# Placing a set's slots one turn later in a graph-layer kernel on one Trainium2 core

## The chip, the cores and the metric

The kernel runs on one core of one Trainium2 chip. The metric is the time of one execution on the device in microseconds (us), the median of several runs. Beside those runs one execution was taken with the hardware profiler; its rows are what the working uses.

## The reference

A graph layer of 12,500 nodes with 128 features and 400,000 edges, sorted by the node that they end in, followed by a residual sum and a normalisation:

```
Xs = X[src]
m_data = Xs @ W_data.T + b_data
m_ctrl = Xs @ W_control.T + b_control
msg = jnp.where((edge_types == 0)[:, None], m_data, m_ctrl)
agg = jax.ops.segment_sum(msg, dst, num_segments=X.shape[0])
out = relu(agg + (X @ W_self.T + b_self))
x = layernorm(x + out)
```

The kernel adds the rows of x per node and edge type first, and multiplies by the weights afterwards.

## The kernel before

The 3,125 columns of 128 edges are cut into 25 groups (g) of 125 columns, and each group into five pairs of windows. The short window of a pair ("p", 5 columns, once 25) fetches its source rows from DRAM by GpSimd's indirect DMAs (L725). The long one ("e", 20 columns, 2,560 edges) fetches nothing: x lies in SBUF as three bf16 parts (x3), and TensorE picks the rows with one-hot matrices. The loop at L1010 makes one step for each of the 113 e-windows ("sets", w).

Picking needs a table of slots: for each of 100 cells (blocks of 128 nodes) up to 32 edges. `give_slots` (L523) makes it for one set:

- VectorE (DVE) builds the one-hot block matrix O (L531) and sums of it (`fours`, L547, L548); TensorE adds them along the lanes into the PSUM tile rk (`before`, L555); VectorE makes the rank of each edge within its cell (`ranks`, L565 to L580), and from it a one-hot rank matrix times node and code, rv (`rank_matrix`, L603 to L607).
- `put` (L614) places the slots: 20 matmuls of O and rv into rk (L619).
- `spread` (L624) casts rk to bf16 on ScalarE (ACT; tile cell, L627), writes its 100 x 32 node part to DRAM (tile there, L629) and reads it back into all 128 partitions (tile pick, 800 KB, L631). Both transfers go through SyncE's queue (SP).
- `turn_codes` and `keep_codes` (L636 to L650) move the code part into the tile code, by small matmuls from cell (L639) and one ScalarE cast (L649). With them goes the third and fourth part of `spare_slots`, for the few edges that found no slot (L507, L514 to L518).

rk has one buffer, so the next set's `before` can begin when `keep_codes` has read it. pick has two, one in use and one being filled. VectorE then turns pick into the one-hot matrix in place, in two halves (`pick_matrix`, L661).

A step of the loop holds six turns (`unit(t)`, t = 0 to 5, in `picked`, L823) for its own set w. Turn t picks 4 x 128 rows in 16 matmuls each for two PSUM tiles (got, L790), which ScalarE casts to emsg (L802); VectorE makes the one-hot matrix of codes (esel, L784); TensorE counts (L814) and adds the rows of the turn before into the window's sums (L821, shown as L676). The last turn, t = 5, also picks the last rows (L808, into the tile fin or got) and counts the last five. At the end of a turn it runs `tiled.get(t)`, which are parts of the set w + 2; those under 6 run in `end`, which is called in turn 0 of the next step. Other work is merged into the step by due times: `before` in turn 1, `ranks` at 0.26, `rank_matrix` at 0.3, the block matrix of set w + 3 at 0.55, `pick_matrix` of set w + 1 at 0.6 and 0.65, p-windows, loads, and about once in four to five steps the `finish` of an earlier group (fp32 products L918, normalisation on VectorE, L947 on ScalarE, output L950, and reads of x rows, L890).

The framework's scheduler takes the instructions in that order as priorities and fixes at build time in which order each engine gets them; an engine works in its own order and waits by semaphore. The order in the trace differs from the listed one where the scheduler saw a gap: the first half of pick_matrix (L661) usually stands between L569 and L574 of `ranks`, though it is listed after both.

Of the kernel before, what the change touches and what calls it, by code (L numbers as in the profile page):

```python
# [150 lines left out]
def short_path(ctx, tc, const, ident, eps, wT, brow, bad, x, src, dst, etype, ws, bs, out):  # L151
# [371 lines left out]
    def give_slots(w):  # L523
        g, i = each_e[w]
        blk, blk2, node2, code2, pk = (t[:, i * EC:(i + 1) * EC] for t in codes["e", g])
        s = {}
# [122 lines left out]
            nc.scalar.copy(code, at.to_broadcast(list(code.shape)))  # L649
            s["spares"][3]()  # L650

        s["tiled"] = {4: [put, spread], 6: [turn_codes, keep_codes]}
        return s, [(0.58, block_matrix), (0.6, fours), (0.66, same_lane)], [
            (0.1, before), (0.26, ranks), (0.28, lambda: s["spares"][1]()), (0.3, rank_matrix), (0.75, over),
        ]
# [302 lines left out]
    def last_spares():  # L958
        s = spare_slots(pairs - 1, ps1.tile([P, 512], FP, name="rk"))
        return {6: s[2:]}, [(0.1, s[0]), (0.28, s[1])]  # L960

    def begin_slots(w):
        slots[w], a, b = give_slots(w)
        begun[w] = b
        return [u for _, u in a]
# [44 lines left out]
    for w in range(pairs):  # L1010
# [9 lines left out]
        tiled, begin = {}, []  # L1020
        if w + 2 < pairs:
            tiled, begin = slots[w + 2]["tiled"], begun.pop(w + 2)
        elif w + 2 == pairs:
            tiled, begin = last_spares()
# [184 lines left out]
```

## Time and profile before

| | before |
|---|---|
| median of 3 runs | 1956.54 us (1954.3 to 1966.5) |
| profiled execution, own time | 1946.23 us |
| its span, first to last instruction | 1944.4 us |
| mean granted TensorE clock | 0.986 |
| TensorE matmul (PE) busy | 1753.1 us, 90% |
| TensorE weight load (PEld) busy | 1354.9 us, 70% |
| VectorE (DVE) busy | 1717.1 us, 88% |
| GpSimd (POOL) busy | 1362.6 us, 70% |
| ScalarE (ACT) busy | 1303.0 us, 67% |
| DMA, mean | 131 GB/s |

The busy shares in 40 slices are even from the third slice to the last but one: the main loop fills the span. A row of the groups or of the timeline gives line, engine, operation, tiles written and read, and shape; "idle" or the bracket at the end of a row is how long the engine stood before it, and what released it. SPq is SyncE's queue, on which DMAs are issued.

### The profile page before, as it was taken

What the parts mean: (1) busy time and instruction counts of PE and PEld (TensorE: products, weight loads), DVE (VectorE), ACT (ScalarE), POOL (GpSimd) and SP (SyncE); (2) the same over time, 40 slices, a digit from 0 to 9 for tenths busy, and PEclk for the clock granted to TensorE, in tenths of its full rate; (3) what the DMA queues carried; (4) which work ended last, traced back from release to release, by engine and by line L of the source; (5) the groups of instructions that cost most, each with busy time, mean ns of one, the idle gap of its engine ahead of it and who ended that gap; (6) DMA issues with size and microseconds to landing.
All of it is one profiled execution on the core that took longest, in us unless ns stands there. A gap on an engine that the chain in (4) does not pass through costs nothing.

```text
span 1944.4 us, 75191 instructions
## 1 busy us (share of the span) xinstructions
PE 1753.1 (90%) x30869; PEld 1354.9 (70%) x30869; DVE 1717.1 (88%) x4707; ACT 1303.0 (67%) x2464; POOL 1362.6 (70%) x996
## 2 busy tenths in 40 slices
PE   0669999999999999999999999999999999999996
PEld 0457777677777776777777777777777777777775
DVE  7969999999899888999999889989989889888883
ACT  4646776676676676676676667667676666766765
POOL 0378768777788777667777667787787667777760
PEclk9989999999999999999999999999999999999998
DMA  7734443443543443443444434444434344444331
GB/s 210 227 94 129 134 148 108 144 147 101 149 141 107 145 136 110 145 136 115 140 136 119 123 129 119 143 127 126 144 129 146 114 128 144 117 136 135 115 111 35
DMA packets 186533, 254.91 MB, mean 131 GB/s; under 512 B 85369, under 2 KB 152995, under 8 KB 183108
## 3 DMA queue, kind: packets, MB, share of 16 engines
q1 hardware_dynamic: 128418, 152.97, 24.6%
q0 software_dynamic: 45136, 90.65, 16.5%
q10 hardware_dynamic: 12626, 6.40, 1.2%
q8 instruction: 243, 3.98, 0.8%
q14 instruction: 110, 0.90, 0.1%
HBM read 231.89 MB, written 18.04 MB: 129 GB/s over the span
## 4 chain that ended last, share of the span: by engine, by line
DVE 53%; PE 30%; DMA 10%; issue 3%; ACT 2%; DVEq 1%; SPq 1%; POOL 0%; ACTq 0%
PE sums L676 13%; PE got L790 8%; DMA pick<-there 7%; DVE esel L481 6%; DVE pick L661 6%; DVE prod L569 5%; DVE rv L607 4%; DVE found L578 3%; DVE prod L547 3%; PE rk L619 3%; DVE half L574 3%; DVE ahead L565 3%; DVE rm L481 2%; DVE half L575 2%; DVE prod L548 2%
## 5 line engine op out<-in xcount | busy, mean ns | idle before, releaser
L725 POOL DMA_INDIRECT msg<-rows,pidx x865 | 1212.8, 1402 | 376.8 <-PE got L790 163.0
L802 ACT CAST emsg<-got 128x768 bf16<-128x768 f32 x1356 | 1026.9, 803 | 356.5 <-PE got L790 337.0
L676 PE MATMUL sums<-esel,emsg 128*128 128x176 bf16 x8136 | 748.2, 241 | 0.0
L676 PEld LDWEIGHTS <-emsg 128*128 128x128 bf16 x8136 | 596.2, 98 | 156.0 <-issue 143.2
L790 PE MATMUL got<-x,pick 128*32 128x384 bf16 x10896 | 611.6, 331 | 12.6 <-ACT emsg L802 10.1
L790 PEld LDWEIGHTS <-pick 128*32 128x32 bf16 x11074 | 250.0, 96 | 125.3 <-issue 20.3
L481 DVE TENSOR_TENSOR esel<-code_col,code 128x1408 bf16<-128x1408 bf16 x339 | 309.0, 912 | 8.8 <-PE sums L676 3.2
L769 POOL DMA_INDIRECT last<-rows,idx x113 | 145.7, 1289 | 171.7 <-DMA bias<-b_parts 70.9
L676 PE MATMUL sums<-psel,msg 128*128 128x48 bf16 x2595 | 184.9, 185 | 7.3 <-DVE acc L714 5.1
L714 DVE TENSOR_TENSOR acc<-acc,sums 128x352 f32 (+2 forms) x238 | 101.4, 426 | 96.9 <-PE sums L676 81.6
L619 PE MATMUL rk<-rv,O 128*128 128x64 bf16 x2260 | 89.6, 195 | 103.3 <-DVE rv L607 103.0
L619 PEld LDWEIGHTS <-O 128*128 128x128 bf16 x2260 | 86.1, 100 | 127.8 <-issue 126.6
L814 PE MATMUL sums<-esel,one_col 128*32 128x176 bf16 x2825 | 169.5, 242 | 2.1 <-DVE esel L481 1.2
L676 PEld LDWEIGHTS <-msg 128*128 128x128 bf16 x2595 | 149.2, 97 | 15.9 <-issue 13.3
L661 DVE TENSOR_SCALAR pick<-pick,lane_f 128x1600 bf16<-128x1600 bf16 x226 | 144.1, 643 | 17.0 <-DMA pick<-there 16.5
L761 PE MATMUL sums<-psel,one_col 128*128 128x48 bf16 x865 | 145.3, 183 | 0.0
L481 DVE TENSOR_TENSOR O<-cell_col,blk 128x2000 bf16<-128x2000 bf16 x113 | 134.2, 1188 | 4.9 <-issue 2.5
L569 DVE TENSOR_TENSOR prod<-O,ahead 128x2000 bf16<-128x2000 bf16 x113 | 134.1, 1187 | 0.0
L814 PEld LDWEIGHTS <-one_col 128*32 128x32 bf16 x2825 | 80.9, 96 | 34.0 <-issue 2.2
L565 DVE TENSOR_REDUCE ahead<-rk 128x100 bf16<-128x500 f32 x113 | 76.0, 673 | 12.0 <-PE rk L497 9.0
L627 ACT CAST cell<-rk 128x64 bf16<-128x64 f32 x113 | 23.9, 212 | 87.9 <-PE rk L619 79.1
L761 PEld LDWEIGHTS <-one_col 128*128 128x128 bf16 x865 | 82.8, 96 | 0.0
(173 smaller groups left out, 2077.0 us busy)
## 6 DMA issues: line engine op xcount, KB each, us to landing
pick<-there SPq DMA_DIRECT2D x113, 800.0 KB
acc<-acc_start SPq DMA_DIRECT2D x23, 1280.0 KB
msg<-rows,pidx POOLq DMA_INDIRECT x865
rows<-x SPq DMA_DIRECT2D x6, 1344.0 KB
xs<-in_x_dram SPq DMA_DIRECT2D x99, 62.5 KB
out_dram<-h SPq DMA_DIRECT2D x99, 62.5 KB
xt<-in_x_dram ACTq DMA_DIRECT2D x6, 896.0 KB
there<-cell SPq DMA_DIRECT2D x113, 6.2 KB
```

Source lines behind the costliest of these rows:

```text
L481: nc.vector.tensor_tensor(sel.rearrange("p n (w t) -> p n w t", t=2), col[:rows].rearrange("p (o w t) -> p o w t", o=1, t=2).to_broadcast( ...
L565: nc.vector.tensor_reduce(ahead, s["rk"][:, :CQ * NCELL].rearrange("p (c j) -> p j c", j=NCELL), AX.X, OP.add)
L569: nc.vector.tensor_tensor(prod, s["O"], ahead.rearrange("p (o j) -> p o j", o=1).to_broadcast([P, EC, NCELL]), op=OP.mult)
L619: nc.tensor.matmul(s["rk"][:m, :2 * CAP], s["held"][:, c * NCELL:c * NCELL + m], s["rv"][:, c].rearrange("p v r -> p (v r)"), start=(c == ...
L661: nc.vector.tensor_scalar(t, t, lane_f, None, op0=OP.is_equal)
L676: nc.tensor.matmul(out, msg[:, j * D:(j + 1) * D], sel, start=(start and j == 0), stop=stop, skip_group_check=True)
L725: return nc.gpsimd.indirect_dma_start(out=msg, out_offset=None, in_=rows3[:, :], in_offset=bass.IndirectOffsetOnAxis(ap=codes["p", g][0][: ...
L761: nc.tensor.matmul(cnt, one_col, sel, start=False, stop=(c == n - 1), skip_group_check=True)
L769: return nc.gpsimd.indirect_dma_start(out=msg[:OVF, :], out_offset=None, in_=rows3[:, :], in_offset=bass.IndirectOffsetOnAxis(ap=slots[w][ ...
L790: last = nc.tensor.matmul(ps[CAP * a:CAP * (a + 1), :], slots[w]["pick"][:, a * NQ + q, :], x3[:, 4 * q + a - a0].rearrange("p j d -> p (j ...
L802: nc.scalar.copy(msg, ps[:, :, :3 * D])
L814: nc.tensor.matmul(cells_of(s["ps"], EW, 1)[CAP * (q % 4):CAP * (q % 4 + 1), :], one_col[:, :CAP], s["sel"][q], start=(q < 4), stop=(q + 4 ...
```

## The change

`put` and `spread` of set w + 2 are run at the end of turn 5 of step w instead of turn 4. In the listed order they come after the picking, counting, last rows and adding of turn 5 and no longer before them. Nothing else is changed, and no instruction is added or dropped.

```diff
-        s["tiled"] = {4: [put, spread], 6: [turn_codes, keep_codes]}
+        s["tiled"] = {5: [put, spread], 6: [turn_codes, keep_codes]}
```

The parts that it moves, as they stand:

```python
        def put():
            for c in range(EC):
                m = P if c < EC - 1 else NCELL
                nc.tensor.matmul(
                    s["rk"][:m, :2 * CAP], s["held"][:, c * NCELL:c * NCELL + m], s["rv"][:, c].rearrange("p v r -> p (v r)"),
                    start=(c == 0), stop=(c == EC - 1), skip_group_check=True,
                )

        def spread():
            cell = s["cell"] = two.tile([P, 2 * CAP], BF, name="cell")
            nc.scalar.copy(cell, s["rk"][:, :2 * CAP])
            there = scr.tile([NCELL, CAP], BF, name="there")
            nc.sync.dma_start(out=there[:, :], in_=cell[:NCELL, :CAP])
            pick = s["pick"] = two.tile([P, NCELL, CAP], BF, name="pick")
            nc.sync.dma_start(
                out=pick.rearrange("p j r -> p (j r)"),
                in_=there.rearrange("(o j) r -> o (j r)", o=1).to_broadcast([P, NCELL * CAP]),
            )
```

## The prediction, made before the result was known

> **What bounds the kernel now.** I read the page first. Its engine rows and the chain that ended last say that neither TensorE nor VectorE rules alone:
>
> ```profile
> PE 1753.1 (90%) x30869; PEld 1354.9 (70%) x30869; DVE 1717.1 (88%) x4707; ACT 1303.0 (67%) x2464; POOL 1362.6 (70%) x996
> DVE 53%; PE 30%; DMA 10%; issue 3%; ACT 2%; DVEq 1%; SPq 1%; POOL 0%; ACTq 0%
> ```
>
> Two engines at about 90% that hold the chain in turn are two that wait for each other. The list of waits (who waited for whom: total us, times, longest) names the places:
>
> ```profile
> PE rk L619 <- DVE rv L607: 103.0, 83, 19.0
> DVE acc L714 <- PE sums L676: 81.6, 62, 13.5
> DVE pick L661 <- DMA pick<-there: 16.5, 22, 2.2
> ```
>
> TensorE stands before `put` until VectorE has made rv; VectorE stands before `accumulate` until TensorE has closed the sums; and VectorE stands a little for the transferred pick. The first and the third row are the two ends of the moved step. The chain of waits in order of time shows how they lie in one ordinary step (start, us, what):
>
> ```profile
> 1842.15 0.81 DVE rv L607 x2
> 1842.97 0.04 issue
> 1843.01 0.76 PE rk L619 x20
> 1843.77 0.19 PE got L790
> 1843.96 0.23 PE sums L814 x8
> 1844.20 0.16 PE fin L790 x2
> 1844.36 1.09 PE sums L676 x15
> ...
> 1848.99 0.34 PE rk L555 x4
> 1849.33 0.05 PE rk L497
> 1849.38 0.02 issue
> 1849.40 0.68 DVE ahead L565
> ```
>
> So a step is two phases: VectorE from `ahead` to rv, then TensorE from rv to the next `ahead`. In the second one `put` stands first, and behind it in TensorE's queue comes the rest of turn 5: three got, eight counts, the two last rows, twelve sums. That is 0.19 + 0.23 + 0.16 + 1.09 = 1.67 us of work which needs neither rv nor `put`, behind an instruction that waits for rv (0.80 us in this step).
>
> Last I lined up all 113 sets from the timeline: end of rv, start of put, issue of pick, the last of pick's 128 packets of 6,400 bytes, first half of pick_matrix. Leaving out the first four sets, where the start lies, and the last, there are two kinds. In 84 ordinary sets put stands in TensorE's queue in the middle or at the end of turn 5's got matmuls and TensorE waits there, 72.2 us in all, 0.86 a set; the step takes 15.1 us (median). In 24 sets the fp32 products of `finish` hold TensorE up, put comes 2.3 us after rv with no wait, and the step takes 20.1 us. One of those:
>
> ```profile
> 1012.66 0.76 PE L619 MATMUL rk<-rv,O 128*128 128x64 bf16 x20
> 1013.46 0.21 ACT L627 CAST cell<-rk 128x64 bf16<-128x64 f32 x1 [0.21 <-PE rk L619]
> 1017.15 0.35 SPq L631 DMA_DIRECT2D pick<-there  x1
> 1019.30 2.62 SPq L192 DMA_DIRECT2D esrc<-in_src_dram  x1
> 1024.00 0.64 DVE L661 TENSOR_SCALAR pick<-pick,lane_f 128x1600 bf16<-128x1600 bf16 x1 [0.66 <-DMA pick<-there]
> ```
>
> Here VectorE does stand for pick (last row, 0.66 us), though it was issued before the loads of the next group (L192).
>
> **The change, part by part.** *Put on TensorE.* Nothing is added. The 20 matmuls (0.76 us) go behind 1.67 us of turn 5. Per set TensorE saves the wait, as far as it is under 1.67 us, and VectorE gains only if it then really stood for TensorE in that phase. The smaller of the two, taken set by set (wait before put; VectorE's idle time before L714, L518 and L565), sums to 45 us over the 84 sets, 0.53 each. Its ends: 0, if the scheduler keeps put where it is, and 68 us, if every wait under 1.67 us turns into time. In the other 24 sets there is no wait to save: 0.
>
> *Spread on ScalarE.* One cast of 0.21 us goes behind the cast of the last rows (0.47 us) and perhaps one of emsg (0.80 us). In a few sets it already starts 0.8 us late. On `turn_codes` it has no effect: after put come turn 0's 16 got (0.76 us) and 15 sums (1.24 us) before L639 wants cell, which is 2.0 us of cover against 0.3 for the cast. For pick it costs 0 to 0.8 us.
>
> *Spread's transfers on SP.* From the start of put to pick's last packet it takes 7.2 us (median of the ordinary sets; 1.6 of it from there to pick's issue, 4.2 from that issue to the last packet); the first halving starts 8.9 us after put. Less 0.35 us, the smallest time seen between last packet and halving, 1.3 us are free (median; under that in 42 of the 84). The change eats them from both sides: put starts later by 1.6 less the wait, 0.79 us on average, and the halving wants to start 0.53 us sooner. If VectorE's order stays as it is, it stands 30 us over the 84 sets, leaving 15 of the 45.
>
> In the 24 finish sets put falls behind all of turn 5, since it stood ahead of turn 5's got: from its end to the end of those twelve sums are 2.7 us (median). Pick has next to nothing free there, so with VectorE's order unchanged it stands 57 us more. A bound below is 0, if the halving is seated later. A bound above is 103 us, if pick falls behind the loads on SP too (4.6 us a set, from two issues of esrc of 2.62 and 1.95 us). Pick's own reuse costs nothing: the buffer's last readers, the last rows, now precede put.
>
> *Where VectorE gets the halvings.* This decides, and no row shows it directly. The order is fixed at build time, and the first halving sits between L569 and L574 only when the scheduler counted pick as landed by then. In 15 of the ordinary sets it did not, and both halves stand right after rv, or near it, 6.6 us or more after pick had landed. Put one turn later makes this more frequent. It costs little: after rv VectorE has the idle time of the second phase, and TensorE wants the halves only at turn 0's got, after put; two halves are 1.30 us on VectorE, against put's 0.76 us and what is left of turn 5. It would even shorten the first phase. So I take a third of the 30 us (10) in the ordinary sets and none in the finish sets, the row that 15 sets show.
>
> *GpSimd.* The gathers are released by got matmuls, and got of turn 5 runs in front of put then, so none comes later; GpSimd is busy 70%. 0.
>
> Sum: 1946.2 − 45 + 10 = 1911 us for the profiled execution. The median of the runs is 10.3 us above that execution (0.53%); scaled, 1921 us.
>
> **The rivals.** *Pick becomes the wait; slower.* Mechanism: the scheduler leaves the first halving between L569 and L574, and VectorE, in its order, stands there for a transfer that now starts later, with `ranks` and so the next rv queued behind it. Price: 30 + 57 − 45 = +42 us, so 1999; with SP's loads in front, more. It decides once the stands exceed the 45 us gained, which is 0.4 us a set. For it: in the finish sets the halving already waits (10.6 of the 16.5 us lie there), so the scheduler's view of that transfer is too short. Against it: the 15 sets in which it was moved. The Trainium skill has a rule against this change, in DMA: Bandwidth & Descriptors, Rules for kernel authors: issue the transfer early and wait for it late, so that its fixed cost is covered; by that rule this rival is the outcome, and the trace bears it out as far as 22 waits go.
>
> *Given back.* Ordinary sets save 45 and pay 30, finish sets pay 0 to 30: between −15 and +15 us, 1941 to 1972. The same time results, from 0 us, if the scheduler fills put into the same gap as now, so that the change does not do what it says. Against that: the rest of turn 5 has all it needs while TensorE waits.
>
> *TensorE takes it all.* Halvings after rv shorten the first phase too, until TensorE never waits at put: −68 us, 1888. Against it: in some 20 sets VectorE has no idle time in the second phase.
>
> **How the numbers follow.** About 1% is what a measurement of this kernel can tell from no change (its runs spread 0.6%). Forecast (1900 to 1937) 0.36; all of TensorE's wait 0.07; given back 0.20; pick the wait 0.37. The two signs hold almost equal chances. Faster by over 1% (under 1937) 0.43, within 1% 0.20, slower 0.37. The range that leaves out 2 in 10 reaches from the second case to the slower rival's price: 1890 to 1999; the forecast's own is 1900 to 1937.
>
> **What would show it.** Right: TensorE's wait at L619 for rv falls from 103 us to under 45 (31 lie in the first two sets); put stands behind turn 5's twelve sums; VectorE's wait at L714 falls by 40 or more; L661's wait for pick stays under 35; more halvings lie after L607. Wrong: L661's wait above 60 us, or, in the finish steps, pick's issue behind L192. The forecast falls if the first halving stays between L569 and L574 in most steps.

## The result, and the profile after

The changed kernel takes 1934.39 us (median of 5 runs, 1924.73 to 1936.75), the kernel before, on the same chip, 1954.3 us (median of 5, 1948.21 to 1966.5). The ratio is 0.9911, with a 95% interval of 0.9882 to 0.9941: 0.9% faster, between 0.6 and 1.2%. The profiled execution after is that of 1924.73 us, the fastest of its five, with a span of 1922.7 us and a granted clock of 0.99 (before 1946.23, 1944.4 and 0.986). The forecast was 1921 us; its own range, 1900 to 1937, holds the result, which lies at the edge of the 1% that was called a difference.

The page after, engine rows and the shares of the chain that ended last:

```profile
PE 1738.0 (90%) x30869; PEld 1348.3 (70%) x30869; DVE 1718.7 (89%) x4707; ACT 1287.1 (67%) x2464; POOL 1309.6 (68%) x996
DVE 49%; PE 22%; DMA 16%; issue 5%; ACT 4%; POOL 1%; DVEq 1%; SPq 0%; ACTq 0%; POOLq 0%
```

VectorE does the same work (1717.1 us before). On the chain TensorE's share fell from 30 to 22%, and that of the transfers rose from 10 to 16%. The list of waits after (engine and line that stood, and what it stood for: total us, times, longest) says which:

```profile
ACT bits_b L600 <- DVE bits L598: 100.7, 85, 5.0
...
DVE pick L661 <- DMA pick<-there: 47.4, 42, 3.7
...
PE rk L619 <- DVE rv L607: 31.8, 5, 19.0
PE sums L676 <- DVE acc L714: 28.0, 37, 1.9
PE got L790 <- ACT emsg L802: 27.4, 67, 1.8
...
DVE acc L714 <- PE sums L676: 24.5, 23, 11.0
```

Two of these rows before the change:

```profile
ACT bits_b L600 <- DVE bits L598: 29.7, 53, 5.0
...
PE sums L676 <- DVE acc L714: 5.1, 8, 1.8
```

TensorE's wait before `put` fell from 103.0 to 31.8 us, and what is left lies in the first sets. VectorE's wait for the sums fell from 81.6 to 24.5. Its wait for pick rose from 16.5 to 47.4. The first row is new at this size: ScalarE standing in front of its cast bits_b. TensorE gave back part of what it saved: it stands 23 us more before its sums, for VectorE's acc, and 17 more for emsg (10.1 before).

How the first and the second row belong together is seen in one step after. The chain of waits in order of time (start, us, what):

```profile
974.80 0.28 DVE bits L598
...
975.33 0.22 ACT cell L627
975.57 1.39 DMA there<-cell
...
977.02 4.92 DMA pick<-there
...
981.97 0.64 DVE pick L661
```

The cast cell reads rk, which TensorE wrote, but the chain comes to it from VectorE's bits. The timeline of the same step shows why (start, us, engine, line, what; in brackets how long the engine stood, and for what):

```profile
972.85 0.76 PE L619 MATMUL rk<-rv,O 128*128 128x64 bf16 x20
...
974.78 0.28 DVE L598 TENSOR_SCALAR bits<-top_i 128x8 int32<-128x8 int32 x1
...
975.10 0.21 ACT L600 CAST bits_b<-bits 128x24 bf16<-128x24 int32 x1 [2.22 <-DVE bits L598]
975.33 0.21 ACT L627 CAST cell<-rk 128x64 bf16<-128x64 f32 x1
...
980.14 0.68 DVE L574 TENSOR_TENSOR half<-prod 128x1000 bf16<-128x1000 bf16 x1
...
981.97 0.64 DVE L661 TENSOR_SCALAR pick<-pick,lane_f 128x1600 bf16<-128x1600 bf16 x1 [1.14 <-DMA pick<-there]
...
982.52 0.40 DVE L575 TENSOR_TENSOR half<-half 128x480 bf16<-128x480 bf16 x1
```

ScalarE stood 2.22 us in front of bits_b, with cell queued behind it; put had ended at 973.61, so cell was ready 1.72 us before it ran. The transfer went out late with it, and VectorE then stood 1.14 us for pick, now between L574 and L575, one place later than before.

To see where the 21.5 us went I added up VectorE's time over the 108 steps from rv of set 4 to rv of set 112 in the timelines, cut at each `ahead` (L565). Second phase is from rv to the next `ahead`, first phase from there to the next rv; idle is time in which no VectorE instruction runs.

| us | idle, second phase | idle, first phase | busy | 108 steps |
|---|---|---|---|---|
| before | 144.4 | 18.7 | 1598.6 | 1761.7 |
| after | 88.0 | 53.2 | 1600.3 | 1741.5 |
| difference | −56.4 | +34.5 | +1.7 | −20.2 |

After the change VectorE is idle 56.4 us less in the phase where it stands for TensorE and 34.5 us more in the one where it stands for pick. Of the first, 48.8 us lie in the 84 ordinary steps and 7.6 in the 24 finish steps; of the second, all (35.4 and −0.9) in the ordinary ones.

The 56.4 us are not `put`'s work alone. The cut at `ahead` stands still while VectorE's work moves across it: most halvings now come after rv, and 40.1 us of busy time have moved from the first phase into idle time of the second. The second phase itself is shorter by 16.3 us (830.9 to 814.6) and the first by 3.9 (930.8 to 926.9).

### The profile page after: what moved, and what is told of

Its sections match the earlier page's. It is cut to its first block, busy times and chain, and to the rows that moved or that the text cites. A ratio compares the mean times of both kernels' runs of the same rounds, so it can differ in the third digit from the quotient of the medians.

```text
span 1922.7 us, 75198 instructions
## 1 busy us (share of the span) xinstructions
PE 1738.0 (90%) x30869; PEld 1348.3 (70%) x30869; DVE 1718.7 (89%) x4707; ACT 1287.1 (67%) x2464; POOL 1309.6 (68%) x996
## 4 chain that ended last, share of the span: by engine, by line
DVE 49%; PE 22%; DMA 16%; issue 5%; ACT 4%; POOL 1%; DVEq 1%; SPq 0%; ACTq 0%; POOLq 0%
DMA pick<-there 11%; PE sums L676 10%; DVE esel L481 8%; PE got L790 6%; DVE pick L661 5%; DVE rv L607 4%; DVE found L578 3%; DVE prod L547 3%; DVE prod L569 2%; ACT emsg L802 2%; DMA there<-cell 2%; DVE rm L481 2%; DVE acc L714 2%; PE rk L619 2%; DVE half L575 2%
## 5 line engine op out<-in xcount | busy, mean ns | idle before, releaser
L725 POOL DMA_INDIRECT msg<-rows,pidx x865 | 1171.1, 1354 | 383.0 <-issue 164.1
L790 PE MATMUL got<-x,pick 128*32 128x384 bf16 x10896 | 598.2, 331 | 30.2 <-ACT emsg L802 27.4
L769 POOL DMA_INDIRECT last<-rows,idx x113 | 134.4, 1189 | 196.7 <-DVE om L503 72.5
L661 DVE TENSOR_SCALAR pick<-pick,lane_f 128x1600 bf16<-128x1600 bf16 x226 | 143.2, 648 | 47.9 <-DMA pick<-there 47.4
L814 PE MATMUL sums<-esel,one_col 128*32 128x176 bf16 x2825 | 161.8, 241 | 24.6 <-DVE esel L481 17.1
L569 DVE TENSOR_TENSOR prod<-O,ahead 128x2000 bf16<-128x2000 bf16 x113 | 133.6, 1182 | 0.0
L714 DVE TENSOR_TENSOR acc<-acc,sums 128x352 f32 (+2 forms) x238 | 100.7, 423 | 35.3 <-PE sums L676 24.5
L619 PE MATMUL rk<-rv,O 128*128 128x64 bf16 x2260 | 89.8, 196 | 31.9 <-DVE rv L607 31.8
L619 PEld LDWEIGHTS <-O 128*128 128x128 bf16 x2260 | 85.8, 101 | 35.0 <-issue 32.8
L600 ACT CAST bits_b<-bits 128x24 bf16<-128x24 int32 x113 | 24.0, 212 | 102.3 <-DVE bits L598 100.7
L574 DVE TENSOR_TENSOR half<-prod 128x1000 bf16<-128x1000 bf16 x113 | 76.4, 676 | 2.4
```

Of the source, the lines that this page charges most:

```text
L569: nc.vector.tensor_tensor(prod, s["O"], ahead.rearrange("p (o j) -> p o j", o=1).to_broadcast([P, EC, NCELL]), op=OP.mult)
L619: nc.tensor.matmul(s["rk"][:m, :2 * CAP], s["held"][:, c * NCELL:c * NCELL + m], s["rv"][:, c].rearrange("p v r -> p (v r)"), start=(c == ...
L661: nc.vector.tensor_scalar(t, t, lane_f, None, op0=OP.is_equal)
L714: added.append(nc.vector.tensor_add(win, win, ps[:, :4 * wide].rearrange("p (a w) -> p a w", w=wide)[:, :, :width]))
L725: return nc.gpsimd.indirect_dma_start(out=msg, out_offset=None, in_=rows3[:, :], in_offset=bass.IndirectOffsetOnAxis(ap=codes["p", g][0][: ...
L769: return nc.gpsimd.indirect_dma_start(out=msg[:OVF, :], out_offset=None, in_=rows3[:, :], in_offset=bass.IndirectOffsetOnAxis(ap=slots[w][ ...
```

## The experiments

All were timed beside the kernel before. It took 1952.56 us (17 runs) beside the first four below and 1948.61 (17 runs) beside before_bits_after_cell, before_halves_after_rv and both; beside the other four it took 1949.32 (11 runs). Ratios are to that kernel. Waits and idle times come from one profiled execution of each kernel. Lines in their profiles are shifted by one or two where the edit adds lines.

**over_late.** First theory for the grown wait: `over`, due at 0.75 of the step, now has its cast bits_b (L600) in front of cell. The edit makes it due later.

```diff
-(0.3, rank_matrix), (0.75, over),
+(0.3, rank_matrix), (0.95, over),
```

> The changed kernel with one number more: `over` is listed at 0.95 of the step instead of 0.75, so behind put and spread. Theory A (ScalarE's queue): in the changed kernel the cast of cell stands behind the cast bits_b, which waits for VectorE's `over`, in 78 of 108 sets, and starts 0.96 us after put on average instead of 0.13; that delay is what made the wait for pick grow to 47 us. Then here cell starts under 0.4 us after put on average, VectorE's wait for pick falls under 30 us, and the time is 1910 to 1925 us. Theory B (put's own place): pick is late because put is late, the cast matters little; then the wait stays over 40 us and the time stays at 1930 to 1938 us.

Measured: 1928.6 us, ratio 0.9885 (0.9848 to 0.9922), indistinguishable from the change. Wait for pick 47.8 us, as after. The edit did not do what it should: bits_b still stands ahead of cell in 42 of the 108 sets (78 after). The due time is only a priority, and the scheduler puts bits_b in where it counts it ready. Inconclusive on the theory.

**finish_at_4.** The slower rival of the prediction had its highest price in the finish steps. Here put and spread stay in turn 4 in steps that carry a `finish`, and only there.

```diff
+            if rest:
+                tiled = {4 if t == 5 else t: u for t, u in tiled.items()}
```

> The changed kernel, but in the steps that carry a `finish` (24 of the 108) put and spread stay in turn 4. If the finish steps cost what the slower rival said (put later there with no wait of TensorE to save), the time is 10 to 25 us under the changed kernel's 1934: 1909 to 1924 us. If the loss lies in ordinary steps, or the scheduler has seated the halvings later in finish steps at no cost, it is 1930 to 1940 us.

Measured: 1933.05 us, 0.991 (0.9875 to 0.9946). The same as the change, so the finish steps cost it nothing. Its profiled execution, 1945.05 us, is the longest of its six, so its wait for pick (61.4 us) is no fair comparison.

**only_finish_at_5.** The opposite: only the finish steps are changed.

```diff
+            if not rest:
+                tiled = {4 if t == 5 else t: u for t, u in tiled.items()}
```

> The other part alone: put and spread in turn 5 only in the steps with a `finish`, in turn 4 elsewhere. TensorE waits before put only in ordinary steps, so this part should gain nothing: TensorE's wait at L619 stays at 95 to 105 us and the time is 1950 to 1975 us (kernel before: 1954). If it is under 1945 us, the gain of the change does not come from the wait before put.

Measured: 1945.6 us, 0.9964 (0.9944 to 0.9985). Its waits stay those of before:

```profile
PE rk L619 <- DVE rv L607: 103.5, 84, 19.0
...
DVE pick L661 <- DMA pick<-there: 17.1, 15, 2.8
```

A late put in the finish steps is no loss; it gains 0.4%, where nothing was expected of it. The 57 us feared there do not exist.

**after_old_there.** The change, with pick read from the part that the set before wrote, so that the read-back need not wait for this set's write to DRAM (rows are picked by another set's slots).

```diff
+            theres.append(there)
...
-                in_=there.rearrange("(o j) r -> o (j r)", o=1).to_broadcast([P, NCELL * CAP]),
+                in_=theres[max(0, len(theres) - 2)].rearrange("(o j) r -> o (j r)", o=1).to_broadcast([P, NCELL * CAP]),
```

> The changed kernel, where pick is read from the node part that the set before has written to DRAM, so that its transfer waits neither for put nor for cell; rows are thus picked by another set's slots. All sizes and counts stay. It shows what the change gives once pick's latency is taken out: VectorE's wait for pick near 0, TensorE's wait at L619 as in the changed kernel. If the 31 us more that VectorE waits for pick are what is missing from the forecast, the time is 1895 to 1915 us. If it stays at 1925 to 1935 us, that wait was covered by something else.

Measured: 1911.35 us, 0.9796 (0.9764 to 0.9829): some 23 us under the change by the medians. In the ordinary sets pick's last packet now lies 4.13 us after rv (9.34 after the change), 5.2 us sooner. But the first halving came forward with it, from 11.73 to 6.83 us after rv, and VectorE's wait for pick fell only from 47.4 to 34.3 us, not to nearly 0 as expected. Of what is left, nearly all now lies in the second phase.

**before_old_there.** The same in the kernel before.

> The kernel before, with pick read from the node part that the set before has written (the rows picked are another set's). With pick's latency out of the way on both sides, this against the changed kernel so treated (1911 us) is what the moved put alone gives. If put's place is worth the 45 us of the forecast's first term, this takes 1945 to 1960 us; if it is worth only about 20, it takes 1925 to 1937 us and the shorter latency is worth the rest.

Measured: 1970.33 us, 1.0106 (1.007 to 1.0142), slower than either expectation, and the wait for pick rose from 16.5 to 38.7 us although pick is there 1.5 us sooner in the ordinary sets (5.86 us after rv for 7.33). The timeline shows where the scheduler put the halvings:

```profile
963.87 0.62 DVE L662 TENSOR_SCALAR pick<-pick,lane_f 128x1600 bf16<-128x1600 bf16 x1
...
964.41 0.66 DVE L565 TENSOR_REDUCE ahead<-rk 128x100 bf16<-128x500 f32 x1
965.32 1.19 DVE L569 TENSOR_TENSOR prod<-O,ahead 128x2000 bf16<-128x2000 bf16 x1
966.43 0.62 DVE L662 TENSOR_SCALAR pick<-pick,lane_f 128x1600 bf16<-128x1600 bf16 x1
```

The first half now stands in front of `ahead`. It came 1.3 us forward (from 10.10 to 8.83 us after rv), and the next rv waits in line behind it. So the seat (the place that the scheduler gives an instruction in its engine's order) seems to follow the landing that the scheduler counts on, and in both kernels that is earlier than the real one. The wait for pick is a matter of the seat at least as much as of the transfer.

The two kernels with the older part also give a price for `put`'s place. Their halvings are seated nearly alike (the first half stands after rv in 89 and 87 sets), their waits for pick are 38.7 and 34.3 us, and placing the slots in turn 5 saves 59 us (1970.33 to 1911.35), above the 45 expected. The second phase is shorter by 58.6 us there and the first longer by 3.5.

**bits_after_cell.** The first theory again, with a tie in place of a due time: bits_b is given to ScalarE only behind cell (`issue_after` keeps an instruction behind a named one in the order of its engine).

```diff
-            nc.scalar.copy(s["bits"], bits)
+            with tc.issue_after(s["cell_in"].ins) if "cell_in" in s else ExitStack():
+                nc.scalar.copy(s["bits"], bits)
...
-            nc.scalar.copy(cell, s["rk"][:, :2 * CAP])
+            s["cell_in"] = nc.scalar.copy(cell, s["rk"][:, :2 * CAP])
...
-(0.3, rank_matrix), (0.75, over),
+(0.3, rank_matrix), (0.95, over),
```

> The changed kernel with the ScalarE order forced: `over` listed at 0.95 and its cast bits_b tied behind the cast of cell. In the changed kernel 50 of 108 sets have cell directly behind bits_b, 1.35 us late each; listing `over` later alone left 38 of them. Theory A (the cast's place on ScalarE makes the new wait for pick): cell behind bits_b in no set, VectorE's wait for pick falls from 47 to 15 to 30 us, time 1905 to 1922 us. Theory B (the wait is set by put's own place and by where the scheduler seats the halving): wait for pick still 40 to 60 us, time 1925 to 1937 us.

Measured: 1913.06 us, 0.9808 (0.9766 to 0.9851), about 20 us under the change by the medians; the spans of the profiled executions differ by 11 (1911.6). Its waits:

```profile
ACT bits_b L601 <- DVE bits L598: 52.2, 64, 5.0
...
DVE pick L662 <- DMA pick<-there: 31.9, 27, 2.9
```

After the change bits_b stands directly ahead of a late cell in 50 sets, which then starts 1.35 us after put on average. Here cell starts within 0.3 us of put's end in 77 sets (38 after the change), the sum of its delays falls from 103 to 37 us, and the wait for pick by 15.5. The time is as theory A has it, the wait a little above its 15 to 30: half of the rise from 16.5 to 47.4 is left.

**before_bits_after_cell.** The control: the same tie in the kernel before, where bits_b stands directly ahead of a late cell in 3 sets only.

> The kernel before, with the cast bits_b given out behind the cast of cell, as in bits_after_cell. There bits_b stands directly ahead of a late cell in 3 sets only (50 after the change). Theory A, bits_after_cell gained because cell no longer stands behind bits_b on ScalarE: here there is next to nothing to take away, time 1945 to 1953, pick's wait stays at 13 to 18 us. Rival B, it gained by bits_b's later place itself (ScalarE free for emsg, TensorE's bits products later): then it gains here too, 1925 to 1940, with pick's wait unchanged.

Measured: 1951.05 us, 1.0005 (0.9983 to 1.0026). Nothing, so the tie gains where ScalarE's queue had grown and not by itself. (Its wait for pick, 24.0 us, came out higher than either theory said; the time does not show it.)

**halves_after_rv.** The seat of the halvings alone: the change, with both halves of pick tied behind rv, which is where the prediction thought a late pick would send them.

```diff
-                nc.vector.tensor_tensor(
+                s["rv_last"] = nc.vector.tensor_tensor(
...
-            nc.vector.tensor_scalar(t, t, lane_f, None, op0=OP.is_equal)
+            with tc.issue_after(slots[w + 1]["rv_last"].ins) if "rv_last" in slots.get(w + 1, {}) else ExitStack():
+                nc.vector.tensor_scalar(t, t, lane_f, None, op0=OP.is_equal)
```

> The changed kernel with both halves of pick_matrix tied behind the last rv product of the same step (seat as in 24 of its sets, now in all). Theory of the forecast (a later seat costs nothing and saves the wait): VectorE's wait for pick under 5 us, the phase from ahead to rv shorter by about 1 us in ordinary steps, time 1885 to 1910 us. Rival: the picked rows of the next step's turn 0 then wait for the halves on TensorE, about 0.5 to 1 us in each of 108 steps; time 1930 to 1980 us.

Measured: 1875.05 us (1873.49 to 1878.42), 0.9616 (0.9583 to 0.9649). The wait for pick in the 108 sets is 0.03 us, and the time lies below the 1885 to 1910 expected. The chain and one step of the timeline:

```profile
DVE 56%; PE 27%; issue 5%; ACT 4%; DMA 4%; DVEq 2%; POOL 1%; SPq 1%; ACTq 0%; POOLq 0%
```

```profile
959.48 0.48 DVE L607 TENSOR_TENSOR rv<-rm,code 128x640 bf16<-128x640 bf16 x1
959.88 1.29 DVE L662 TENSOR_SCALAR pick<-pick,lane_f 128x1600 bf16<-128x1600 bf16 x2
...
961.67 0.76 PE L619 MATMUL rk<-rv,O 128*128 128x64 bf16 x20
```

Both halves run while TensorE does the rest of turn 5, and `put` has no wait in its row. Without the tie the first half had this seat in 43 sets, not in the 24 that the expectation names. The transfers' share of the chain is down to 4%.

**halves_after_found.** The tie a little earlier, behind the sum `found` (L578) instead of rv.

```diff
-            nc.vector.tensor_reduce(found, half[:, :, :26], AX.X, OP.add)
+            s["found_in"] = nc.vector.tensor_reduce(found, half[:, :, :26], AX.X, OP.add)
...
+            with tc.issue_after(slots[w + 1]["found_in"].ins) if "found_in" in slots.get(w + 1, {}) else ExitStack():
```

> The same with the halves tied behind the reduction `found` only (L578), so that they stand before the rank matrix and rv. Their 1.1 us stay in the phase from ahead to rv. Forecast's theory: wait for pick under 10 us, time 1895 to 1915 us. If the wait for pick is covered anyway by TensorE's work, the time stays at 1930 to 1937 us.

Measured: 1878.65 us, 0.9636 (0.9602 to 0.9669), below its 1895 to 1915 too. Nearly all halves come to stand behind rv here too (in the 108 steps 4.3 us of halvings lie in the first phase, 0.0 with the tie behind rv), so it tells little apart.

**before_halves_after_rv.** Is the seat a gain of its own? The kernel before, put in turn 4, with the halvings behind rv.

> The kernel before (put and spread in turn 4), with the halvings of pick tied behind rv, as in halves_after_rv. Theory A, the two things add up: the seat of the halvings is worth some 60 us wherever put stands, and the change's own part (TensorE's wait at put) stays as it was: L619 still waits for rv by 80 us or more, time 1890 to 1900, and halves_after_rv at 1875 beats it by 15 to 25 us. Theory B, the seat takes the same wait away: with the halvings behind rv the first phase of a step is 0.6 to 0.7 us shorter, rv comes before TensorE reaches put, L619's wait falls under 60 us, and putting the slots one turn later is worth nothing more: 1870 to 1883. Theory C, the seat pays only where the slots are placed late: 1930 or more, VectorE's wait at L714 grows.

Measured: 1905.82 us, 0.9771 (0.9748 to 0.9793). Its waits:

```profile
PE rk L619 <- DVE rv L607: 77.5, 82, 19.0
...
DVE acc L715 <- PE sums L677: 47.4, 46, 7.6
```

The seat alone gains 43 us (2.3%), without any change to the transfer. The result fits none of the three theories to the number; theory A, the two add up, comes nearest. Of TensorE's wait at put, 46 of 72 us remain in the 108 sets, and putting the slots one turn later takes them away: from 1905.82 to 1875.05 is 30.8 us, with the second phase shorter by 32.7 us and the first longer by 1.3. With pick's wait out of the way the placing in turn 5 is thus worth 31 us, with it 20.

**both.** The two ties together with the change.

> The kernel after, with both ties: bits_b behind cell on ScalarE, and the halvings of pick behind rv. Theory A, cell's delay on ScalarE costs time only through VectorE's wait for pick: with the halvings behind rv that wait is 0 already, so bits_after_cell adds nothing, 1872 to 1880 as halves_after_rv (1875). Rival B, the two add up, because the late cast holds ScalarE or TensorE up as well: 1850 to 1862.

Measured: 1874.65 us, 0.9605 (0.9581 to 0.9629), the same as halves_after_rv. The late cell on ScalarE costs time only through VectorE's wait for pick; where that is gone, it costs nothing.

VectorE's account over the same 108 steps for the kernels that separate the parts:

| us | idle, second phase | idle, first phase | busy | 108 steps |
|---|---|---|---|---|
| after | 88.0 | 53.2 | 1600.3 | 1741.5 |
| bits_after_cell | 90.3 | 39.3 | 1602.3 | 1732.0 |
| before_halves_after_rv | 104.6 | 8.7 | 1609.9 | 1723.2 |
| halves_after_rv | 74.3 | 9.6 | 1608.1 | 1691.9 |

The tie behind cell takes 14 us from the first phase's idle time and nothing from the second's. The seat behind rv empties the first phase, and fills idle time of the second with work that had stood in the first.

## Why the prediction was right, and where a size was off

*Put on TensorE: the mechanism is right, the size fits but is not measured alone.* The term was 45 us, from the smaller of TensorE's wait and VectorE's idle time in each ordinary set. Put stands behind turn 5's sums in all 108 sets, the wait at L619 fell to 31.8 us (forecast: under 45), the wait at L714 by 57 (forecast: 40 or more). VectorE's idle time in the second phase fell by 48.8 us in the ordinary steps and by 7.6 in the finish steps, but halvings that moved in fill part of it, so this is not put's price. Where the halvings keep their seats, later slots are worth 31 us (both halves behind rv) or 59 us (the older part read), and in both pairs it is the second phase that gets shorter. The 45 us lie between; for the seats of the two kernels of the forecast no run parts put from the halvings.

*Pick: the mis-sized term.* The sum had +10 us for it, "a third of the 30 us (10) in the ordinary sets". VectorE's idle time in the first phase rose by 35.4 us there (its wait for pick by 33.8), more than the 30 us for an order that does not change at all. Two things were in it.

First, the seat. The first half did leave its place, as said: between L569 and L574 it stood in 77 of the 113 sets before and in none after. But in 58 sets it went only one place on, to between L574 and L575, which is 0.6 us later; after rv, before the next `ahead`, it stands in 43 (15 before). The second halves went there in 111 (41 before). The wait sits at the seat in between: of the 47.1 us in the 108 sets, 46.0 lie in those 58, and 1.0 in the 41 of the 108 with the first half after rv. The prediction took the 15 sets with both halves near rv as the pattern for a late pick and had no price for a seat in between. That a seat after rv costs nothing, its reason for the small term, is what halves_after_rv shows most strongly.

Second, the transfer came later than worked out. In the ordinary sets pick's last packet lies 9.34 us after rv, 7.33 before: 2.0 us, where 0.79 was put down for put and "0 to 0.8 us" for ScalarE's queue was named but left out of the sum. Put itself starts 1.06 us later, and cell another 0.73 us after put's end. The ScalarE step looked at the casts of emsg and of the last rows. What made cell late was neither: in 50 ordinary sets it was bits_b, itself waiting for VectorE, and in 18 finish sets the normalisation's activation h (L947). Behind h cell was late by 1.62 us on average, but only 1.0 us of the wait for pick lies in those 18. Moved behind an instruction that waits, cell took over that wait, and this one was not on the list. The Trainium skill says in Perfetto Trace Analysis, Per-instruction lifecycle, that ScalarE and VectorE work through their queues strictly in order; the timeline agrees, with cell ready for 1.72 us behind a bits_b that waits for VectorE.

bits_after_cell prices the late cell: 14 us of the first phase's idle time, of which 7.6 lie in the ordinary steps and 6.3 in the finish steps, and 11 (spans) to 20 us (medians) of the time. Of the 35.4 us that is about a fifth, and a rough figure: in before_bits_after_cell the wait for pick moved by 7.5 us without a trace in the time. The seat is the larger part: with both halves behind rv the whole wait goes, though cell is late by 0.81 us on average there too.

*The finish steps: right.* "None in the finish sets", since the halvings there are seated later: the first half stands after rv in 19 of the 24 (in none before), and idle time in the first phase changed by −0.9 us.

*Sum.* −56.4 for −45, +34.5 for +10, +1.7 in busy time for 0, and −1.3 outside these steps (the span fell by 21.7 us in all): −21.5 us, from 1946.23 to 1924.73, against the −35 forecast. Against the terms the gain is larger by 11 us and the loss by 24.5. The two are not independent, since the halvings that left the first phase fill idle time of the second; that they cancel as far as they do was not worked out, and to that extent the nearness of 1921 to 1934 is luck.

*The rivals.* "Pick becomes the wait" is the right mechanism at 35 us instead of 87, under the 45 us from which it decides. The rule that stood with it (the Trainium skill, DMA: Bandwidth & Descriptors, Rules for kernel authors: issue early, wait late) agrees with the wait, which rose from 16.5 to 47.4 us with the later issue, but it does not decide the time: the kernel that issues later is faster by 20 us, since `put` no longer holds TensorE up. Waiting later, at the same place of issue, took another 59. "Given back" is wrong in its placing, not much in its size: what is given back is 61% of the idle time gained (34.5 of 56.4). "TensorE takes it all" had its condition right: with the halvings after rv TensorE's wait at put in the 108 sets is 0.0 us.

*The signs.* The wait at L661 was to stay under 35 us, wrong above 60: at 47.4 it lies between, and rightly says that this term was the weak one. "The forecast falls if the first halving stays between L569 and L574": it left.

One sign of being wrong did appear. Pick's issue lies behind L192 in 17 of the 24 finish steps, and in none before. The step of the prediction's example, after the change:

```profile
1011.04 0.32 SPq L629 DMA_DIRECT2D there<-cell  x1
1011.46 0.41 SPq L192 DMA_DIRECT2D esrc<-in_src_dram  x1
...
1014.38 0.35 SPq L631 DMA_DIRECT2D pick<-there  x1
```

It cost nothing that shows: idle time in the first phase of these steps changed by −0.9 us. The load is issued behind `there`, whose landing the issue of pick waits for in any case, and its issue takes 0.41 us here, for 2.62 before. From the issue of `there` to that of pick it is 3.65 us on average in the finish steps, 3.57 before. The sign had the place right and the price wrong.

What is not shown: why the scheduler counts pick as landed too early. Its times were not to be seen, only its seats; that it goes by a too short transfer is inferred from the two kernels with the older part, where an earlier transfer drew the halvings forward into a new wait.

## What to carry to other kernels

Ask of a moved step which waits it now stands behind on every queue it passes: the cast in front of cell had nothing to do with the moved data and was itself waiting. When a transfer becomes later, look where its consumer stands in its engine's order before looking at the transfer: tying two instructions to a place after the work that others wait for was worth twice the change (43 us alone, 59 on top of it). And a scheduler's order can hold a wait of its own making: here a later due time left 42 of 78 casts in front of cell, an earlier transfer left 34 of the 47 us of waits for pick, and the tie to a place in the order removed them.

## What was not expected of the hardware

The transfer of pick took as long as before in the ordinary sets (4.25 us from issue to last packet, 4.28 before), but in the finish sets 4.43 us for 5.46. Two experiments tie this to the place of put in those steps: with put kept in turn 4 there (finish_at_4) it took 5.58 us, with put in turn 5 there alone (only_finish_at_5) 4.19. What held it up at the earlier place, perhaps the finish's own transfers, is not shown.
